# First image's group statistics formed and spread by TensorE instead of by way of DRAM

## The chip, the cores and the metric

The kernel runs on one core of a Trainium2 chip, as one launch. The metric is the device time of one execution in microseconds, as the median of several runs. All tensors are float32.

## The reference

Two layers of the same form act on four images of 32 x 32 positions with 768 channels. Each layer adds to its input the output of a multi-head self-attention (12 heads of 64) with relative position biases. The attention's input is normalized by groups of channels. Cut to what matters here:

```python
def _gn(v, G=32, eps=1e-5):
    g = v.reshape(B_, H_, W_, G, C_ // G)
    m = jnp.mean(g, axis=(1, 2, 4), keepdims=True)
    s = jnp.var(g, axis=(1, 2, 4), keepdims=True)
    return ((g - m) / jnp.sqrt(s + eps)).reshape(v.shape)

# attention of a layer, on the normalized input
qkv = x @ Wqkv                                # layer 1 also adds a bias
scores = scale * q @ k.T + bias               # bias[q, k] = rel_h + rel_w
out = softmax(scores) @ v
return out @ Wproj + bproj

x = x + _L0_conv_ref(_gn(x), ...)
x = x + _L1_conv_ref(_gn(x), ...)
```

A group is 24 neighbouring channels over all 1024 positions. Its variance is the mean of the 24 channels' variances plus the variance of their 24 means.

## The kernel before

An image is held with channels in the partitions: 768 channels are six blocks (`c`) of 128, and each block is two tiles of 512 positions (`h`). Layer and image together give eight images `im`, and each has six pairs of heads. A unit of the main loop is one pair and one block of 128 query positions (384 units). In a unit TensorE forms scores, VectorE adds the bias that GpSimd has written (L429), ScalarE takes the exponentials, VectorE transposes blocks of 32, two DMAs by way of DRAM complete the transposition, and TensorE weighs the values (`weigh`, L508). Beside this, TensorE projects queries, keys and values of the next pair (`products`, `project_values`, through `crossed`, L285) and the outputs. GpSimd forms combinations of weights (`combine`, L126) and of inputs (`sums`, L243), which the products use.

The order of the work is written out by hand under a manual schedule. What stands ahead of it, the loads and the tables of positions, is placed by the framework. The DMAs of weights and inputs are on SP's queue. Tiles come from rotating pools: `pt` and the PSUM pool `m` have two buffers each, `nrm` has two.

The work around the change is at the start, for image 0 alone. VectorE takes the statistics of each channel as the tiles land (`stats`, L188 and L191) and leaves mean and variance in `mv_of[0]`. Groups of 24 channels cross the partitions, and 128 is no multiple of 24, so the kernel sends the 768 x 2 numbers to DRAM (`gather`) and reads them back with a group in each of 32 partitions (`by_group`). VectorE and ScalarE form a factor and an offset for each group (`groups`, `inverses`). The two are copied 24 times, written to DRAM, and read back with a channel in each partition (`spread`). Then `apply` normalizes the twelve tiles in place, six on VectorE and six on ScalarE, and TensorE's first products begin:

```python
stages, apply = norm(0)
for n in sorted(stages):
    stages[n]()
for stage in range(2):
    combine(0, stage)
for h in range(2):
    for c in range(NC):
        apply(c, h, c % 2 == 1)
```

The four DMAs of image 0 are on ScalarE's queue. For images 1 to 7 the same stages run on SP's queue, spread over units of the pair before, and with other work beside them.

## Time and profile before

| | |
|---|---|
| median of 3 runs | 3404.13 us (3402.43 to 3408.83) |
| profiled execution | 3401.86 us, its span 3400.0 us |
| PE busy | 3324.9 us, 98% of the span |
| VectorE, ScalarE, GpSimd busy | 2347.4, 2090.8, 2332.3 us |
| chain that ended last | PE 81%, DMA 7%, DVE 4%, ACT 4% |
| last channel statistics end | 13.52 us |
| first normalization begins | 26.80 us |
| first matmul | 27.40 us |

The busy times are of the whole span; the last three rows are read from the chain of waits, with times from the span's start. The names PE, PEld, DVE, ACT, POOL and SP in the profile are TensorE's matmuls, its weight loads, VectorE, ScalarE, GpSimd and SyncE. L191 is line 191 of the kernel.

### The profile page before, as it was taken

The numbers are of one execution on the slowest core, as the hardware profiler recorded it, in microseconds if no ns is written. First come the engines' busy times: TensorE is split into PE (matmuls) and PEld (weight loads), VectorE is DVE, ScalarE is ACT, GpSimd is POOL, SyncE is SP. The second block draws the span as 40 slices with busy tenths as digits, with TensorE's granted clock in tenths as the row PEclk, the third lists the DMA queues.
The fourth block names the chain that finished last, engine by engine and source line by source line (L and its number), as shares of the span: only waits on it lengthen the run. The fifth ranks groups of instructions, "written<-read, shape, count | busy, mean of one in ns | idle before, by whom it ended". The sixth has DMA issues, their size and how long they took to land.

```text
span 3400.0 us, 58086 instructions
## 1 busy us (share of the span) xinstructions
PE 3324.9 (98%) x21600; PEld 1877.2 (55%) x21600; DVE 2347.4 (69%) x3826; ACT 2090.8 (61%) x3237; POOL 2332.3 (69%) x1184
## 2 busy tenths in 40 slices
PE   6999999999999999999999999999999999999998
PEld 3555555555555555555555555555555555555554
DVE  3776677766777666766767766666766676666675
ACT  2666756566566666566665666666666667665663
POOL 5776866668666686666866668666686667766662
PEclk9999999999999999999999999999999999999999
DMA  3898989999998998889888989989988999898887
GB/s 112 307 325 300 335 298 337 321 304 327 317 318 316 318 324 309 309 297 332 313 309 311 312 311 320 317 310 315 325 314 305 332 299 335 308 311 301 312 292 259
DMA packets 534777, 1046.97 MB, mean 308 GB/s; under 512 B 149728, under 2 KB 212704, under 8 KB 485344
## 3 DMA queue, kind: packets, MB, share of 16 engines
q1 hardware_dynamic: 479936, 1015.84, 85.3%
q10 hardware_dynamic: 54560, 27.43, 2.8%
q8 instruction: 171, 2.80, 0.3%
q14 instruction: 110, 0.90, 0.1%
HBM read 568.01 MB, written 475.10 MB: 307 GB/s over the span
## 4 chain that ended last, share of the span: by engine, by line
PE 81%; DMA 7%; DVE 4%; ACT 4%; issue 2%; POOL 1%; SPq 1%; ACTq 0%; DVEq 0%; POOLq 0%
PE pj L285 20%; PE s L443 16%; PE av L508 14%; PE pv L285 13%; PE oo L285 12%; DMA td<-tb 5%; PE pj L313 3%; PE tp L381 2%; DVE tb L479 2%; ACT sc L473 2%; POOL sc L429 1%; PE o L587 1%; ACT sc L459 1%; DMA xn<-in_x 1%; ACT xn L233 1%
## 5 line engine op out<-in xcount | busy, mean ns | idle before, releaser
L429 POOL TENSOR_TENSOR sc<-rel 128x1024 f32<-128x1024 f32 x768 | 1879.7, 2476 | 660.1 <-DVE tb L479 626.8
L455 DVE CUSTOM_DVE_ANT_0 sc<-s,sc 128x1024 f32<-128x1024 f32 x768 | 910.8, 1225 | 747.9 <-PE s L443 561.9
L459 ACT ACTIVATE sc<-sc,sm 128x1024 f32<-128x1024 f32 x768 | 878.7, 1146 | 472.0 <-DVE sm L455 471.0
L473 ACT ACTIVATE sc<-sc,sm 128x1024 f32<-128x1024 f32 x674 | 743.0, 1143 | 581.2 <-DVE sm L467 415.4
L479 DVE STREAM_TRANSPOSE tb<-sc 128x1024 f32<-128x1024 f32 x768 | 909.9, 1227 | 52.8 <-DMA td<-tb 44.7
L443 PE MATMUL s<-k,q 64*128 64x512 f32 x3072 | 738.3, 596 | 1.7 <-DVE sm L455 1.7
L508 PE MATMUL av<-pt,v 128*64 128x256 f32 x6144 | 685.5, 381 | 7.0 <-DMA pt<-td 6.0
L508 PEld LDWEIGHTS av<-pt,v 128*64 128x64 f32 x6144 | 434.8, 137 | 287.0 <-issue 45.0
L285 PE MATMUL pv<-wv,xn 64*128 64x256 f32 x4608 | 522.8, 376 | 1.0 <-DVE wv L274 1.0
L285 PEld LDWEIGHTS pv<-wv,xn 64*128 64x128 f32 x4608 | 447.3, 187 | 114.1 <-issue 56.9
L285 PE MATMUL oo<-attn,wo 64*128 64x512 f32 x2112 | 477.1, 591 | 0.0
L443 PEld LDWEIGHTS s<-k,q 64*128 64x128 f32 x3072 | 290.1, 187 | 313.7 <-issue 292.2
L285 PEld LDWEIGHTS oo<-attn,wo 64*128 64x128 f32 x2112 | 202.0, 188 | 228.7 <-issue 227.2
L471 POOL TENSOR_SCALAR sc<-sc,sm 128x1024 f32<-128x1024 f32 x94 | 105.1, 1118 | 311.8 <-DVE sm L467 310.8
L285 PE MATMUL pj<-xn,wa 64*128 64x512 f32 x1152 | 269.1, 598 | 33.2 <-DVE xn L235 27.4
L285 PE MATMUL pj<-xn,w 64*128 64x512 f32 x1152 | 263.4, 589 | 1.6 <-DVE w L274 1.6
L285 PE MATMUL pj<-s,w 64*128 64x512 f32 x576 | 262.7, 589 | 1.5 <-ACT attn L519 0.8
L285 PE MATMUL pj<-s,wc 64*128 64x512 f32 x576 | 262.8, 589 | 0.0
L285 PEld LDWEIGHTS pj<-xn,wa 64*128 64x128 f32 x1152 | 113.6, 189 | 168.9 <-issue 127.4
L285 PEld LDWEIGHTS pj<-xn,w 64*128 64x128 f32 x1152 | 112.4, 187 | 136.6 <-issue 134.1
L404 ACT COPY rel<-raw 32x256 f32<-32x256 f32 x384 | 155.1, 404 | 22.2 <-DMA part<-res 6.7
L285 PEld LDWEIGHTS pj<-s,wc 64*128 64x128 f32 x576 | 107.4, 187 | 67.0 <-issue 67.0
(68 smaller groups left out, 2111.4 us busy)
## 6 DMA issues: line engine op xcount, KB each, us to landing
td<-tb SPq DMA_DIRECT2D x384, 1024.0 KB, 6.5
pt<-td SPq DMA_DIRECT2D x382, 1024.0 KB, 8.9
tdr<-t ACTq DMA_DIRECT2D x96, 256.0 KB, 6.3
part<-res SPq DMA_DIRECT2D x84, 256.0 KB, 4.5
res<-part SPq DMA_DIRECT2D x84, 256.0 KB, 4.9
wa<-in_wqk SPq DMA_DIRECT2D x48, 384.0 KB, 3.2
wc<-in_wqk SPq DMA_DIRECT2D x48, 384.0 KB, 7.4
wv<-in_wv SPq DMA_DIRECT2D x24, 768.0 KB, 12.2
```

The lines of the kernel that those rows point to most:

```text
L285: nc.tensor.matmul(to, lhsT=w, rhs=x, start=(half, at) == (0, 0), stop=(half, at) == (1, n - 1))
L313: nc.tensor.matmul(t[:, h, :], lhsT=w[rows, c, :], rhs=x[c][rows, :], start=(c == 0), stop=(c == NB - 1),)
L381: nc.tensor.matmul(ps[:, h, j, :], lhsT=q[rows, at * P : (at + 1) * P], rhs=tabs[l][rows, :], start=True, stop=True,)
L404: nc.scalar.copy(rel[rows, :, 0, :, :], raw[rows, :, :, WIDE - 1 - HW - y : WIDE - 1 - y])
L429: nc.gpsimd.tensor_tensor(sc.rearrange("p (a k) (u l) -> p a (k u) l", a=4, l=8), rel[:, h, 0, m, :].unsqueeze(1).unsqueeze(3).to_broadcas ...
L443: nc.tensor.matmul(ps[h][:, cols], lhsT=q[rows, n * P : (n + 1) * P], rhs=k[rows, cols], start=True, stop=True,)
L455: nc.vector.tensor_tensor_reduce(out=sc, in0=ps[h], in1=sc, scale=-scale, scalar=BIG, op0=ALU.add, op1=ALU.min, accum_out=st[:, 0, h : h + 1],
L459: nc.scalar.activation(sc, sc, AF.Exp, bias=st[:, 0, h : h + 1], scale=-1.0, accum_out=st[:, 1, h : h + 1],)
L471: nc.gpsimd.tensor_scalar(sc, sc, st[:, 2, h : h + 1], 1.0, ALU.mult, ALU.mult)
L473: nc.scalar.mul(sc, sc, st[:, 2, h : h + 1])
L479: nc.vector.transpose(tb[:, :, h, :], sc_of[g, n, h])
L508: nc.tensor.matmul(av[rows, at * 2 * P : (at + 1) * 2 * P], lhsT=v_of[g][:, k, rows], rhs=pt_of[g, quarter].rearrange("p n r k h i -> p (n ...
```

## The change

Two masks of 0 and 1 are written by GpSimd at the very start, each 128 partitions x 6 x 128. The first, `of_group`, tells for each block of channels which group a channel is in (of 128 columns 32 stand for groups; the rest are empty). The second, `to_channel`, is its transpose by blocks. Each is a memset and two selects. They lie in a buffer of the pool `pt`.

For image 0 the stages by way of DRAM are replaced by four rounds of six matmuls. The first sums the channels' means by group. VectorE divides by 24, and the second round spreads the group's mean to its channels. VectorE forms each channel's variance plus the square of its distance from the group's mean. The third round sums these by group; VectorE and ScalarE form the factor and the offset; the fourth round spreads the two to the channels, and a copy puts them into `nrm`. For images 1 to 7 nothing changes but that SP's queue is now named directly. `apply` is moved into a function of its own.

```diff
+    masks = ptpool.tile([P, 2, 4, NT, 2, HW], FP, tag="pt", name="masks")
+    masks = masks.rearrange("p n r k h i -> p (n r k h i)")
+    of_group = masks[:, : NC * P].rearrange("p (c g) -> p c g", c=NC)
+    to_channel = masks[:, NC * P : 2 * NC * P].rearrange("p (c j) -> p c j", c=NC)
+    for mask, steps, per_row in ((of_group, (P, -GS), 1), (to_channel, (P, 1), -GS)):
+        nc.gpsimd.memset(mask, 1.0)
+        for sign, base in ((1, 0), (-1, GS - 1)):
+            nc.gpsimd.affine_select(
+                out=mask, in_=mask, pattern=[[sign * steps[0], NC], [sign * steps[1], P]],
+                compare_op=ALU.is_ge, fill=0.0, base=base, channel_multiplier=sign * per_row,
+            )
+
     for c in range(NC):
         for h in range(2):
             load_x(0, c, h)
...
+    def norm_first():
+
+        mv = mv_of[0]
+        w = small.tile([P, NC, 2], FP, tag="nrm", bufs=2, name="nrm_work")
+        nrm = small.tile([P, NC, 2], FP, tag="nrm", bufs=2, name="nrm_0")
+        ps = ps_m.tile([P, 2, HALF], FP, tag="m", name="groups_0")
+        total = [ps[:, 1, k : k + 1] for k in range(2)]
+
+        def by_group(to, x):
+            for c in range(NC):
+                nc.tensor.matmul(
+                    to, lhsT=of_group[:, c, :], rhs=x(c), start=(c == 0), stop=(c == NC - 1)
+                )
+
+        def by_channel(at, n, x):
+            for c in range(NC):
+                nc.tensor.matmul(
+                    ps[:, 0, at + n * c : at + n * (c + 1)], lhsT=to_channel[:, c, :], rhs=x,
+                    start=True, stop=True,
+                )
+
+        mean = small.tile([P, 2], FP, tag="gm", bufs=1, name="gm_0")
+        inv = small.tile([P, 2], FP, tag="gi", bufs=1, name="gi_0")
+        by_group(total[0], lambda c: mv[:, c, 0:1])
+        nc.vector.tensor_scalar(mean[:, 0:1], total[0], 1.0 / GS, None, ALU.mult)
+        by_channel(0, 1, mean[:, 0:1])
+        off, var = w[:, :, 0], w[:, :, 1]
+        nc.vector.tensor_tensor(off, ps[:, 0, :NC], mv[:, :, 0], ALU.subtract)
+        nc.vector.tensor_tensor(var, off, off, ALU.mult)
+        nc.vector.tensor_tensor(var, var, mv[:, :, 1], ALU.add)
+        by_group(total[1], lambda c: w[:, c, 1:2])
+        nc.vector.tensor_scalar(inv[:, 0:1], total[1], 1.0 / GS, EPS, ALU.mult, ALU.add)
+        nc.scalar.activation(inv[:, 1:2], inv[:, 0:1], AF.Sqrt)
+        nc.vector.reciprocal(inv[:, 0:1], inv[:, 1:2])
+        nc.vector.tensor_scalar(inv[:, 1:2], mean[:, 0:1], inv[:, 0:1], -1.0, ALU.mult, ALU.mult)
+        by_channel(NC, 2, inv)
+        nc.vector.tensor_copy(
+            nrm, ps[:, 0, NC : 3 * NC].rearrange("p (c k) -> p c k", c=NC)
+        )
+        return applied(0, nrm)
...
-        queue = nc.sync if im else nc.scalar
+        queue = nc.sync
...
-        stages, apply = norm(0)
-        for n in sorted(stages):
-            stages[n]()
+        apply = norm_first()
         for stage in range(2):
             combine(0, stage)
         for h in range(2):
```

More of the change, by code (lines that the diff above doesn't have):

```diff
@@ L191, in stats, with applied, apply @@
             nc.vector.bn_aggr(mv_of[im][:, c, :], st[:, c].rearrange("p i s -> p (i s)"))
+    def applied(im, nrm):
+        def apply(c, h, scalar=True):
+            x = xn_of[im][h][c]
+            if scalar:
+                nc.scalar.activation(x, x, AF.Identity, bias=nrm[:, c, 1:2], scale=nrm[:, c, 0:1])
+            else:
+                nc.vector.tensor_scalar(
+                    x, x, nrm[:, c, 0:1], nrm[:, c, 1:2], ALU.mult, ALU.add
+                )
+        return apply
+    def norm_first():
[32 more added lines that the diff above has]
+            nrm, ps[:, 0, NC : 3 * NC].rearrange("p (c k) -> p c k", c=NC)
+        )
+        return applied(0, nrm)
@@ L228, in spread @@
             queue.dma_start(out=nrm, in_=back.rearrange("(c p) s -> p c s", p=P))
-        def apply(c, h, scalar=True):
-            x = xn_of[im][h][c]
-            if scalar:
-                nc.scalar.activation(x, x, AF.Identity, bias=nrm[:, c, 1:2], scale=nrm[:, c, 0:1])
-            else:
-                nc.vector.tensor_scalar(
-                    x, x, nrm[:, c, 0:1], nrm[:, c, 1:2], ALU.mult, ALU.add
-                )
-        return {1: gather, 2: by_group, 4: groups, 5: inverses, 7: spread}, apply
+        return {1: gather, 2: by_group, 4: groups, 5: inverses, 7: spread}, applied(im, nrm)
     sum_tiles = {}
```

## The prediction

> **What bounds the kernel now.** I first read sections 1 and 4 of the page. TensorE is busy for 98% of the span, and the chain that ended last is 81% PE. So the kernel is bound by TensorE in its steady state, and a few small steps at the start can count only if they delay the first matmul: everything later is released by events, so a delay of the first matmul is carried to the end once, and no more than once. I therefore read the chain of waits in order of time over the first 100 us. The gap that the change addresses lies between these lines (start us, length us, what):

> ```profile
> 13.30 0.22 DVE mv L191
> ...
> 13.54 6.16 DMA per<-mv
> ...
> 19.78 1.81 DMA g<-per
> ...
> 22.54 0.21 ACT gmv L218
> ...
> 22.77 0.16 DVE gmv L221
> ...
> 23.39 1.34 DMA back<-g
> 24.73 0.02 issue
> 24.76 2.02 DMA nrm<-back
> 26.77 0.03 issue
> 26.80 0.56 DVE xn L235
> 27.36 0.04 issue
> 27.40 4.64 PE pj L285 x10
> ```

> From the end of the last channel statistics (13.52) to the first normalization (26.80) pass 13.28 us. Four DMAs take 6.16 + 1.81 + 1.34 + 2.02 = 11.33 us of it; small DVE and ACT instructions and the gaps take the other 1.95. Nothing else is on the chain there, and TensorE has not yet run.

> Then I asked the timelines of TensorE's weight loads and of GpSimd for the same stretch (start us, busy us, line, count, idle before):

> ```profile
> 29.27 0.45 PEld L285 LDWEIGHTS pj<-xn,wa 64*128 64x128 f32 x2 [0.40 <-issue]
> 30.12 0.45 PEld L285 LDWEIGHTS pj<-xn,wa 64*128 64x128 f32 x2 [0.40 <-issue]
> 30.96 0.25 PEld L285 LDWEIGHTS pj<-xn,wa 64*128 64x128 f32 x2 [0.39 <-issue]
> 31.39 0.19 PEld L285 LDWEIGHTS pv<-wv,xn 64*128 64x128 f32 x1 [0.18 <-issue]
> ```

> ```profile
> 0.72 0.35 POOL L156 MEMSET tab<- 128x128 f32 x2 [0.29 <-POOLq L882]
> 14.55 0.99 POOL L129 TENSOR_TENSOR w<-wc,wa 128x384 f32<-128x384 f32 x1 [13.49 <-DMA wc<-in_wqk]
> 19.96 0.53 POOL L166 TENSOR_SCALAR tab<-tab 128x128 f32<-128x128 f32 x1
> 28.80 4.13 POOL L257 TENSOR_TENSOR s<-xn,xn 128x512 f32<-128x512 f32 x3 [8.31 <-DVE xn L235]
> ```

> The loads show how fast TensorE is when it wakes: steps of 0.85 and 0.84 us until 30.96, then 0.43. For its first 3.5 us it runs at half speed. GpSimd is idle from about 1.1 to 14.5 us, and again from 20.5 to 28.8.

> [...] 27.40 to 30.96 at half speed. A second case bears on a chain with pauses: in the stretch from 70 to 80 us the mean granted clock is 0.66, after an idle 3.11 us at 70.0. [...]

> **The change, part by part.** Its own base is the profiled execution: 3401.86 us (span 3400.0 and 1.86 around it), which is 2.27 below the median of 3404.13. I work out a difference and apply it to the median.

> *Removed:* the 13.28 us above, with four ACT queue issues (0.40, 0.34, 0.31, 0.38 us), two of them followed by waits. ACT's table load (1.28 us at 20.16) stood behind them in ACT's queue; now ACT can do it in the first microseconds. It was hidden beside a DMA, and stays hidden.

> *Masks:* two memsets and four selects of 128x768 on GpSimd. A memset of 128 elements takes 0.20 and one of a single element 0.10, so 768 come to about 0.7 us. No select is in the trace. The cheapest near row is the GpSimd multiplication by a scalar (L471, 1118 ns for 1024), which gives 0.84 us for 768. [...] The first is needed at 13.5, the second at about 14.4. Their cover is GpSimd's idle time to 14.5; without it the group chain waits, and behind it the combinations of weights (4 x 0.99), the tables, and the sums.

> *TensorE's rounds:* the new chain has four: sum means by group, spread the mean, sum variances, spread the two factors. Each is six matmuls with 128x128 weights and one or two columns moving. The page counts two PE instructions for an fp32 matmul (pj from xn,wa: 1152 for 48 pairs of heads, so 24 where the code has 12), so a round is 12 loads and 12 tiny matmuls. What does one cost? The matmuls of tp (L381) are the nearest: weights of 128 columns too, 128 columns moving, 16 in 1.16 us on two row halves at once; (1.16 - 0.27) / 8 = 0.11 us a step. With one column moving the load must bind, and I keep 0.11 warm and 0.22 at half clock. Adding what the first load delays (0.14) and the last matmul's drain (0.20: a cold 1057 ns for 512 columns against a step of 853), a cold round takes 0.14 + 11 x 0.22 + 0.20 = 2.76 us, a warm one about 0.08 + 11 x 0.11 + 0.17 = 1.46. The first round is nearly off the path: five channel blocks are done before the last aggregate, so two loads and matmuls remain, 0.56 cold.

> *Small steps:* after round 1 one tensor_scalar (0.20, as L222); after round 2 three VectorE operations on 128x6 (0.20 each); after round 3 tensor_scalar 0.20, Sqrt 0.21, reciprocal 0.16, tensor_scalar 0.20; after round 4 a copy, 0.20. That is 1.77; ten handovers at 0.03 add 0.3.

> *Sum, cold:* 0.56 + 3 x 2.76 + 1.77 + 0.3 = 10.9 us against 13.28: a gain of **2.4 us**. If warm throughout: 0.4 + 3 x 1.46 + 2.1 = 6.9, a gain of 6.4. Is it cold? Busy rounds of 2.8 us alternate with pauses of 0.6 to 0.9, about 75 to 80% busy, mostly loads. After the stop at 70 us TensorE was still at half clock from 73.1 until about 78.6 (its 12 matmuls took 5.49 us against 2.7 warm), although it worked from 73.1 on. So I take cold, and keep the warm end for the range.

> *What is late next:* with normalization at 24.4 the first weights are there (issued at 7.3 to 9.1, 4.6 to 7.2 us to landing), and the combinations and tables end at 20.5 as before. The 12 sums keep their distance to the normalization; TensorE's queue holds them 3 us or more after they are ready (s2 ends at 40.3, its first matmul is at 43.66). Rotating one place in the pt, nrm and m buffers costs nothing: the masks, work tile and PSUM tile are read out before the next user comes; the last is released by the copy that itself precedes the normalization. No SP or POOL DMA moves, and per-image normalization of images 1 to 7 is unchanged on SP.

> **The rivals.** *TensorE wakes during the chain* (0.32): if the loads count as activity, rounds 3 and 4 run warm, the chain falls to about 8.3 (5.0 gained), and the first products, whose cold stretch to 30.96 then goes, come up to 0.9 us sooner by my count: the normalization still feeds them. With rounds warm from the start 7.3 in all, and 9 if the missing cold stretch at 72 us adds its 2.7. For it: the high duty. Against: the pauses. Time about 3397, 5 to 9 below before.

> *The masks are late* (0.19), the case on the other side. The second mask decides once it is ready later than 14.4 + 2.4 = 16.8 us: that is a select of over 3.6 us[...]. [...] For it: GpSimd takes 2.4 ns an element with two inputs, and no select is priced by a run. Against: 13 us of free time.

> *The gain is not passed on* (0.07): another start-up resource, such as GpSimd's sums or the DMA of rel, holds the first scores at 63.4. The chain has nothing but PE and its own followers up to there, so I doubt it; the time would be 3404, or a few microseconds more if half-clock loads cost 0.3 us a step (36 x 0.08 = 2.9 lost).

> **How the numbers follow.** The forecast (0.42) is 3404.13 - 2.4, rounded to 3401.7. A measurement of this kernel can tell about 0.2%, or 6.8 us, from no change; so the forecast is "same". Of the waking case I put 0.24 beyond that bound and 0.08 inside; of late masks 0.16 slower and 0.03 inside; of the third 0.05 inside and 0.02 slower. Faster 0.24, same 0.58, slower 0.18. The range goes from 3395.5 (waking, all of it) to 3407.5 (loads at 0.3 us a step, or masks a little late, with the 6 us between the shown runs in mind), and leaves out most of the late-mask case.

> **What would show it.** Right: no DMA between L191's last aggregate and the first normalization, that stretch 10 to 11.5 us long, weight-load steps of about 0.22 us in three rounds, masks done before 13.5, the first pj matmul near 25. Rounds of 1.5 us say that TensorE woke. A first spread matmul that waits for POOL says that the masks were late. The prediction is wrong if the stretch shrinks and the first scores (63.4) don't move with it, or if the time moves by more than the stretch does.

## The result, and the profile after

The changed kernel took 3394.36 us (median of 13 runs, 3386.99 to 3404.66), the kernel before 3403.6 (13 runs beside it, 3398.76 to 3409.07). The ratio is 0.9971, with a 95% interval of 0.9959 to 0.9982: faster by 0.3%, some 9 us where 2.4 were forecast, and below the forecast's range. With three more sets of runs of the same kernel (experiments; 73 runs in all, against 182 of the kernel before) it is 6.8 ± 1.4 us. Where a difference is given with ± here, it is that of the means of the runs, on one chip unless several sets are put together, with 1.96 standard errors. The changed kernel's profiled execution took 3389.95 us (span 3388.2).

The chain of waits after, at the place where the DMAs stood (start us, length us, what):

```profile
13.29 0.22 DVE mv L203
...
13.55 0.60 PE groups L228 x2
...
14.18 0.17 DVE gm L242
...
14.48 2.71 PE groups L234 x12
...
17.61 0.94 DVE nrm_work L247
...
18.59 2.73 PE groups L228 x12
...
22.25 2.73 PE groups L234 x12
...
25.01 0.18 DVE nrm L254
25.21 0.56 DVE xn L212
25.77 0.04 issue
25.82 5.61 PE pj L342 x10
```

No DMA is left between the last aggregate and the normalization. That stretch, 13.51 to 25.21, is 11.70 us long where it was 13.28: the normalization is 1.6 us sooner. Each full round lasts 2.7 us. In an experiment (`e12`) a round of twelve took 1.48 us at a granted clock of 1.00 and 2.73 at 0.50. By that comparison TensorE is at half clock here; this trace's own records of the clock begin only at 31.48 us.

The other microseconds are far from the edit. TensorE's timeline of the kernel before, behind the last scores (start us, busy us, engine, line, operation, count, and in brackets the idle time ahead and what ended it):

```profile
3341.84 2.27 PE L443 MATMUL s<-k,q 64*128 64x512 f32 x8
3345.11 3.67 PE L508 MATMUL av<-pt,v 128*64 128x256 f32 x32 [1.00 <-DVE sum L606]
3350.35 3.67 PE L508 MATMUL av<-pt,v 128*64 128x256 f32 x32 [1.57 <-DMA pt<-td]
3353.95 1.12 PE L587 MATMUL o<-attn,wa 128*128 128x512 f32 x2
```

and of the changed kernel:

```profile
3333.49 2.27 PE L500 MATMUL s<-k,q 64*128 64x512 f32 x8
3336.76 7.13 PE L565 MATMUL av<-pt,v 128*64 128x256 f32 x64 [1.00 <-DVE sum L663]
3343.82 1.13 PE L644 MATMUL o<-attn,wa 128*128 128x512 f32 x2
```

Before, the second half of these 64 matmuls waits 1.57 us for `pt`, the weights that come back from DRAM. After, it does not wait. From the last scores to the span's end are 53.28 us before and 49.80 after. Early on, the timeline before

```profile
67.83 2.16 PE L443 MATMUL s<-k,q 64*128 64x512 f32 x8
73.10 3.78 PE L285 MATMUL pj<-xn,wa 64*128 64x512 f32 x8 [3.11 <-DVE wa L274]
```

and after

```profile
67.30 2.16 PE L500 MATMUL s<-k,q 64*128 64x512 f32 x8
71.77 4.54 PE L342 MATMUL pj<-xn,wa 64*128 64x512 f32 x12 [2.31 <-DVE wa L331]
```

show a stop of 3.11 against 2.31 us. I therefore split each span at three points: the first scores (start of the first VectorE pass over them: 65.57 before, 65.04 after), from there to the ninth unit's scores (62.46 and 60.02), and behind the last scores (53.28 and 49.80). The two stretches differ by 2.4 and 3.5 us, the start by only 0.5. The middle, 3218.7 and 3213.3 us here, lies anywhere between 3210 and 3221 us in the twenty profiles of this case: it scatters by more than the whole gain. Nothing that the diff touches runs in these stretches, and on every engine the instructions follow in the same order there.

One thing does move. The page's list of DMA queues has this line, word for word the same in both kernels:

```profile
q8 instruction: 171, 2.80, 0.3%
```

These are 171 packets of 16 KB. By the queue's name I take them for reads of instructions, and call them reads. In the records they come, on average, at every 256th of TensorE's instructions (159 to 336 apart before, 170 to 361 after). The change puts 99 more TensorE instructions ahead of the first product (43,943 records in its two queues against 43,844; 96 of them are the four rounds), so every later read comes, on average, 99 instructions earlier in the work: the first three begin at 41.5, 64.5 and 88.4 us before, at 33.4, 50.1 and 81.6 after. This is what the experiments had to test.

### The profile page after: what moved, and what is told of

It is laid out like the page before. It is cut to its first block, busy times and chain, and to the rows that moved or that the text cites. A ratio compares the mean times of both kernels' runs of the same rounds, so it can differ in the third digit from the quotient of the medians.

```text
span 3388.2 us, 58184 instructions
## 1 busy us (share of the span) xinstructions
PE 3333.6 (98%) x21648; PEld 1894.1 (56%) x21648; DVE 2347.9 (69%) x3825; ACT 2090.1 (62%) x3237; POOL 2336.8 (69%) x1190
## 3 DMA queue, kind: packets, MB, share of 16 engines
q10 hardware_dynamic: 52896, 27.40, 2.7%
## 4 chain that ended last, share of the span: by engine, by line
PE 80%; DMA 9%; DVE 4%; ACT 3%; issue 2%; POOL 1%; SPq 1%; ACTq 0%; DVEq 0%; POOLq 0%
PE pj L342 19%; PE s L500 16%; PE av L565 14%; PE pv L342 13%; PE oo L342 12%; DMA td<-tb 6%; PE pj L370 3%; PE tp L438 2%; DVE tb L536 2%; ACT sc L530 2%; POOL sc L486 1%; PE o L644 1%; DMA xn<-mid 1%; DMA xn<-in_x 1%; ACT xn L210 1%
## 5 line engine op out<-in xcount | busy, mean ns | idle before, releaser
L536 DVE STREAM_TRANSPOSE tb<-sc 128x1024 f32<-128x1024 f32 x768 | 909.3, 1226 | 41.7 <-DMA td<-tb 33.4
L516 ACT ACTIVATION_READ_ACCUMULATOR sc<-sc,sm 128x1 f32 x768 | 144.4, 188 | 0.0
```

Of the source, the lines that this page charges most:

```text
L516: nc.scalar.activation(sc, sc, AF.Exp, bias=st[:, 0, h : h + 1], scale=-1.0, accum_out=st[:, 1, h : h + 1],)
L536: nc.vector.transpose(tb[:, :, h, :], sc_of[g, n, h])
```

## The experiments

**1. What counts: the scratch, the start, or something else?** `e1` is the changed kernel again. The first suspects were the DRAM addresses (the change removes two scratch tiles, so later scratch lies 16 KB lower) and the number of DMAs. `e2` restores both in the changed kernel, with nobody reading:

```diff
+        per = dram2.tile([C, 2], FP, tag="per", name="per_0")
+        back = dram2.tile([C, 2], FP, tag="back", name="back_0")
...
+        for to, x in unread:   # four, behind the normalization
+            nc.scalar.dma_start(out=to, in_=x)
```

`e3` delays the changed kernel's start by one more round, unread:

```diff
+        by_group(ps[:, 1, 2:3], lambda c: w[:, c, 1:2])
         by_group(total[1], lambda c: w[:, c, 1:2])
```

`e4` gives the kernel before the new addresses: for the first image `per` and `back` are parts of a tile that another user rotates through.

```diff
+            t_of[0] = dram2.tile([S, P], FP, tag="tdr", name="tdr_0")
+            per, back = t_of[0][:C, 0:2], t_of[0][:C, 2:4]
...
-        if i == 0:
+        if i == 0 and g:
```

> The changed kernel, unchanged, as a measure for the others of this call and for a second trace. All theories: 6 to 14 us below the kernel before, with the first scores about 0.5 us earlier. What it tells: which of the later steps of the difference (at 2053 and 3359 us in the first pair of traces) come back and which were chance.

> The changed kernel, and behind the normalization ScalarE's queue also writes four small unread DMAs into the two scratch tensors that the change had removed. Every later scratch tensor in DRAM then lies where it lay in the kernel before (16 KB higher than in the changed one), and the count of DMAs is the old one. Theory A, the gain comes from the start (an earlier first matmul, and what its new phase does to TensorE's clock later): still 9 us below the kernel before, within 3. Theory B, the gain comes from where the scratch lies in DRAM: at most 2 us below. Theory C, the new turn of the rotating PSUM, pt and statistics buffers: 9 us below, as A.

> The changed kernel with one more round of six matmuls ahead of the variances' round, its result unread. The normalization begins 2.7 us later, at about 27.9, and so 1.1 us later than in the kernel before. Theory A (the start): the gain is gone, 0 to 2 us above the kernel before. Theories B and C (scratch place, buffers): 2.7 us above the changed kernel, so 6 to 7 us below the kernel before.

> The kernel before, but the two small scratch tensors of image 0 lie inside the first 512 KB tensor of position products, which isn't written yet. All later scratch then lies in DRAM where it lies in the changed kernel, 16 KB lower; the way by DRAM and all rotating buffers stay. Theory B (scratch place): 7 to 9 us below the kernel before. Theories A and C: within 2 us of the kernel before.

Measured against the kernel before on this chip (mean 3402.4): `e1` −6.1 ± 2.4 us, `e2` −7.1 ± 2.2, `e3` −5.4 ± 2.6, `e4` +1.3 ± 3.5. The scratch's place is out, in both directions, and so is the count of DMAs. `e3` has its first scores 2.4 us later than the kernel before and is still 5.4 us faster: most of the gain is not the start.

**2. The place of the instruction reads.** `e5` adds 24 unread products (96 TensorE instructions) to the kernel before, while it waits for its statistics; `e7` and `e8` add 12 and 40 (48 and 160 instructions). `e6` adds 39 (156) to the changed kernel, which with its own 99 come to nearly 256, a full turn: the reads stand where they stood before.

```diff
+        d = [ps_m.tile([P, S], FP, tag="m", name=f"d{i}") for i in range(2)]
+        for i in range(24):   # e7: 12, e8: 40, e13: 64; e6 and e11: 39
+            x = xn_of[0][0][0]
+            nc.tensor.matmul(d[i % 2][:32, :1], lhsT=x[:, :32], rhs=x[:, :1], start=True, stop=True)
```

> The kernel before, with 24 tiny unread fp32 matmuls (96 TensorE instructions) ahead of its first product, done by about 12 us while TensorE is idle anyway; nothing else moves, and no address changes. The traces show 16 KB reads by the instruction queue at every 256th TensorE instruction; the change puts 99 TensorE instructions ahead of everything and so moves all of these reads against the data DMAs. Theory D, that shift is the larger part of the gain: 5 to 7 us below the kernel before, the first scores where they were. Theory C (the new turn of rotating buffers) and theory A (the start): within 2 us of the kernel before.

> The changed kernel, with 39 tiny unread matmuls (156 TensorE instructions) ahead of its first round, so that with the change's own 99 the shift comes to 255, next to a whole 256, and the instruction reads lie where they lay in the kernel before; the buffers' turn is that of the changed kernel. Theory D: 0 to 3 us below the kernel before. Theory C: 6 to 7 us below.

> The kernel before, with 12 tiny matmuls (48 instructions). Theory D: the time moves by some microseconds, up or down, and the last stall ahead of the last values (pt late by 1.6 to 2.5 us after the last scores, in the kernel before and in the one with new scratch) is gone or smaller, since no instruction read falls at 1.4 us after the last scores. Theories A and C: within 2 us of the kernel before, and the stall stays.

> The kernel before, with 40 tiny matmuls (160 instructions). Theory D: as for 48, the time moves by some microseconds in either direction; together with 0, 48 and 96 it shows how the time depends on the shift. Theories A and C: within 2 us of the kernel before.

Measured (mean before 3400.6): `e5` −2.1 ± 2.7, `e6` −2.5 ± 2.9, `e7` −0.4 ± 2.8, `e8` −0.2 ± 4.2. With the reads moved back, the changed kernel kept 2.5 of its 6.8 us. Moving them forward in the kernel before did not clearly shorten the time. The profiles say more, though each is of one execution, and those of `e5` and of its repeat `e10` below are the fastest of their 14 runs each. `e5` has the changed kernel's stretches (60.30 and 47.93 us) though it still goes by way of DRAM, and `e6` those of before (62.39 and 53.16). The waits of TensorE in `e6` (us, times, longest) have the old stop again

```profile
PE av L565 <- DMA pt<-td: 5.5, 5, 2.0
...
PE pj L342 <- DVE wa L331: 3.3, 1, 3.3
```

and in `e5` it is gone:

```profile
PE av L508 <- DMA pt<-td: 2.7, 3, 1.3
...
PE pj L285 <- DVE wa L274: 2.3, 1, 2.3
```

**3. Again, and TensorE awake.** Both shifts were run once more beside the changed kernel (`e9`). `e12` tests the forecast's rival: 64 unread products (64 columns moving) run ahead of the rounds in the changed kernel, so that TensorE is awake when they begin.

> The changed kernel again, on the chip of the next three, so that the parts can be set against each other there. Theory D: 5 to 8 us below the kernel before, its stretch behind the last scores 50 us long (53 to 54 in the kernel before).

> The kernel before with 96 TensorE instructions more ahead of its first product, as in e5, with the changed kernel beside it. Theory D: at least half of the changed kernel's gain (3 to 6 us below the kernel before), the rest being the earlier start. If the shift is not the cause: within 2 us of the kernel before while the changed kernel is 5 us or more below.

> The changed kernel with its instruction reads moved back, as in e6. Theory D: 3 to 6 us above the changed kernel, 1 to 3 below the kernel before, and again a stretch of 53 us behind the last scores. If the shift is not the cause: as the changed kernel.

> The changed kernel, with 64 unread matmuls (32 weight columns, 64 columns moving, 256 instructions, so a whole read's worth, and the reads lie as in the changed kernel) ahead of the first round, from about 4 to 13 us. They release TensorE's clock before the rounds begin. If the pauses of the chain are short enough to keep it released: rounds of 1.5 instead of 2.7 us, the normalization near 21.5 instead of 25.2, the first products at full speed, and the first scores 4 to 6 us earlier than in the changed kernel; the time 4 to 6 us below it. If small matmuls and weight loads don't count as activity: rounds of 2.7 us and no change.

Measured (mean before 3401.3): `e9` −7.1 ± 3.1, `e10` −1.3 ± 2.8, `e11` −2.5 ± 2.7, `e12` −6.2 ± 2.5. The answer is the same as in the first set: of some 7 us, reads moved back leave 2.5 (against `e9` on the same chip they cost 4.7 ± 3.6), and reads moved alone bring 1 to 2. `e12` has unread products too, but 256 instructions of them, a full turn, and keeps the gain: the products themselves are not what costs `e6` and `e11` theirs. In `e12` TensorE did not stay awake. The stretches of its profile (from:to us, length; busy us and counts of PE, PEld, DVE, ACT and POOL; then the granted clock, the DMA share and GB/s):

```profile
8.00:13.00 5.00, 5.00 (x86) 5.00 (x85) 4.20 (x10) 0.00 (x0) 0.00 (x0) 1.00 1.05 403
13.00:18.00 5.00, 4.02 (x30) 3.75 (x27) 1.85 (x6) 0.00 (x0) 2.76 (x3) 0.76 0.62 204
18.00:25.00 7.00, 5.44 (x24) 5.27 (x24) 1.04 (x6) 0.20 (x1) 1.93 (x4) 0.50 0.00 0
```

It was at full clock to 15.6 us, in the midst of the second round, and then at half clock through two rounds in which it was busy for 5.44 of 7 us. The first round took 1.48 us warm, the last two 2.73 as before.

**4. What else turns, and what the start is worth.** `e13` shifts the reads by 256 (64 products), a full turn. `e14` turns the rotating buffers (`pt`, `m`, `nrm` and the small tiles) by one place in the kernel before, as the change does, with one-column memsets. `e16` makes the rounds shorter, since a group of channels has only one of 32 rows (`inv`, and `mean` from its product with `to_channel` on, likewise on `:NG`):

```diff
-                    to, lhsT=of_group[:, c, :], rhs=x(c), start=(c == 0), stop=(c == NC - 1)
+                    to[:NG], lhsT=of_group[:, c, :NG], rhs=x(c), start=(c == 0), stop=(c == NC - 1)
...
-                    ps[:, 0, at + n * c : at + n * (c + 1)], lhsT=to_channel[:, c, :], rhs=x,
+                    ps[:, 0, at + n * c : at + n * (c + 1)], lhsT=to_channel[:NG, c, :], rhs=x,
```

`e17` is `e16` once more, and `e18` delays the changed kernel's chain on VectorE without touching TensorE's instructions:

```diff
+        for _ in range(48):
+            nc.vector.tensor_copy(mean[:, 1:2], mean[:, 0:1])
         nc.vector.reciprocal(inv[:, 0:1], inv[:, 1:2])
```

> The kernel before, with 64 tiny unread matmuls (256 TensorE instructions, exactly one read) ahead of its first product: a control for the cost of such matmuls, since all later instruction reads fall where they fell before. If they cost nothing: within 2 us of the kernel before. If they cost 2 to 3 us at the start, that is the part of the shift's gain which e5 and e10 did not show.

> The kernel before, with one dummy tile each in the pools of pt, PSUM m and nrm and two small ones, so that all rotating buffers stand as in the changed kernel; five one-column memsets on VectorE are all it adds. Theory C (the buffers' turn is worth what is missing): 2 to 4 us below the kernel before. Theory D without it: within 2 us.

> The changed kernel on the chip of these runs: 5 to 9 us below the kernel before, under every theory.

> The changed kernel, with 32 weight columns instead of 128 in the two rounds that sum by group, and 32 rows in the two that spread. The number of TensorE instructions is the same, so the reads stay. By the step seen in e5 (0.055 us for 32 columns at half clock, 0.22 for 128), the round of the variances takes 0.9 instead of 2.7 us, and the normalization begins at about 23.3 instead of 25.2. If a gain at the start is carried 1:1 to the end: 2 us below the changed kernel. [...]

> The shortened rounds of e16 again, on another chip. If the start is carried 1:1: 8 to 10 us below the kernel before (the changed kernel's 7 and 2 more). If e16's six runs were right: 12 to 15 us below.

> The changed kernel with 48 copies of one column on VectorE between the variances' round and the reciprocal, about 8 us on the chain. Carried 1:1: the first scores 8 us later than in the changed kernel and the time 8 us above it, so 0 to 2 us above the kernel before. If the start hardly matters, because something later waits anyway: still 4 to 7 us below the kernel before.

Measured (mean before 3401.7): `e13` −2.4 ± 3.7, `e14` −0.2 ± 2.8, `e15` (the changed kernel) −6.2 ± 2.3, `e16` −13.9 ± 4.2 from 6 runs; on the last chip (mean before 3402.9) `e17` −8.7 ± 2.9 and `e18` +2.2 ± 2.9. The turn of the buffers shows no gain. A full turn of the reads leaves the stretches as before (61.97 and 52.37). `e18` has its first scores 9.3 us behind the mean of the changed kernel's profiles (64.5) and lost 9.0 ± 3.2 (from −6.8 to +2.2): the start is carried to the end one to one. (`e3`, with its first scores 3.4 us behind that mean, lost only 1.4 ± 2.9, which the noise still allows.)

`e16` beats both kernels on its chip: 0.9957 (0.994 to 0.9974) of the kernel before, and 7.7 ± 4.3 us below the changed kernel. `e17`, at 0.9969 (0.9957 to 0.9982), beats the kernel before; its 8.7 ± 2.9 us are not clearly more than the changed kernel's 6.8 ± 1.4. The chain of waits of `e16` shows where it gains:

```profile
14.20 0.28 PE groups L228 x2
...
14.79 2.70 PE groups L234 x12
...
18.36 0.81 PE groups L228 x12
...
20.05 2.73 PE groups L234 x12
...
23.01 0.56 DVE xn L212
```

The rounds with 32 columns of weights fall to 0.28 and 0.81 us; those with 32 rows but 128 columns stay at 2.7. First scores come at 62.02 and 62.41, some 2.3 us before the changed kernel's. Carried one to one, that would give −6.8 − 2.3 = −9.1: `e17` fits, and `e16` is 4.8 us beyond it, a little more than its interval.

## Why the prediction was wrong

**What held.** The rounds: 2.71 to 2.73 us against 2.76 forecast, the short first one 0.60 against 0.56, and at half clock as chosen. The waking rival fell, and in `e12` dense work ahead of the rounds did not keep TensorE awake through them (granted clock 0.50 from 18 to 25 us). The masks were early: on GpSimd's timeline

```profile
0.79 1.41 POOL L147 MEMSET masks<- 128x768 f32 x2 [0.29 <-POOLq L937]
2.23 3.31 POOL L149 TENSOR_SCALAR_AFFINE_SELECT masks<-masks 128x768 f32<-128x768 f32 x4
5.49 0.34 POOL L168 MEMSET tab<- 128x128 f32 x2
14.43 0.99 POOL L129 TENSOR_TENSOR w<-wc,wa 128x384 f32<-128x384 f32 x1 [8.59 <-DMA wc<-in_wqk]
```

they end at 5.5 us, and after one more memset GpSimd stood idle for 8.6 us. A memset took 0.74 us (0.7 forecast), a select 0.86 (0.84 by the row of the multiplication by a scalar), and the selects begin as the memsets end. One of the tables of positions, forecast to end at 20.5, was formed only by 29.7, among the sums; nothing on the chain waited for it. "A delay of the first matmul is carried to the end once" held too (`e18`).

**One instruction was mis-sized.** The stretch of this profile is 11.70 us, not 10.9. VectorE's timeline has three operations of the same size in a row:

```profile
17.21 0.17 DVE L245 TENSOR_TENSOR nrm_work<-groups,mv 128x6 f32<-128x6 f32 x1 [2.88 <-PE groups L234]
17.41 0.17 DVE L246 TENSOR_TENSOR nrm_work<-nrm_work 128x6 f32<-128x6 f32 x1
17.61 0.93 DVE L247 TENSOR_TENSOR nrm_work<-nrm_work,mv 128x6 f32<-128x6 f32 x1
```

L247 was put at 0.20 and took 0.94. It ended at 18.54. GpSimd's last weight combination (L129, two inputs from SBUF) ran from 17.53 to 18.52. Both inputs of L247 lie in SBUF too, and it ended 0.02 us after the combination. In `e1`, `e3` and `e18` too the instruction of L247 began less than 0.1 us after that combination, took 0.95 to 0.99 us and ended 0.02 us after it. In `e2`, `e6`, `e9`, `e11` and `e15` it began up to 0.03 us before the combination and took 0.17. There the stretch is some 10.95 us, which is the forecast's 10.9, and `e9` and `e15` are the changed kernel itself. So the forecast of the stretch was right except for this one delay, which a few hundredths of a microsecond decide. The forecast priced the three instructions alike, at 0.20 each, without asking what GpSimd did beside them. What makes the one last until the other ends is not shown. In `e16`, whose chain runs a little later, it is L246 that takes 0.40.

**The start gave less than its stretch.** 1.6 us gained at the normalization were 0.5 at the first scores in the two profiles, since by the clock's records TensorE woke at 31.48 us after and at 30.94 before: it started its products sooner, but had 5.7 us of them at half clock instead of 3.5, so most of the gain went into slow products. In both traces the recorded changes of the clock lie 3.41 us or multiples of it apart, but not at the same times from the span's start: the next are to half, from 71.90 to 78.73 before and from 72.44 to 75.85 after. Over the four profiles of the changed kernel (65.04, 64.66, 64.13 and 64.18, mean 64.5) the start gains 1.1 us on the 65.57 before (65.11 and 65.87 in `e4` and `e14`, whose start is that of the kernel before).

**The step that failed** is the sentence that only a delay of the first matmul can count "and no more than once", with every other edit costed at nothing. The prediction named its own refutation: the time moves by more than the stretch does, 6.8 us against 1.6. It left out that 99 instructions more on TensorE's queue shift its instruction reads against the data transfers. With the reads back in their old place and all else of the change kept, 2.5 ± 2.0 us of the gain remain (`e6` and `e11` together), about what was forecast; 4.3 ± 2.4 are gone.

How a read costs is clearest at the stop of TensorE after the first scores. A DMA of 256 KB takes `t` to DRAM there; in the chain of waits before

```profile
64.14 3.10 DMA tdr<-t
```

and after

```profile
63.61 2.30 DMA tdr<-t
```

In the kernel before, a read begins at 64.47, inside this transfer. In all five profiles with a read 0.3 to 0.9 us behind the issue of this DMA, 2.8 to 3.3 us pass from it to the issue of the DMA that reads the result back, and TensorE's stop grows with it; in the fifteen others it is 2.3 us:

| reads | kernels | TensorE's stop, us | first scores to ninth unit's, us | behind the last scores, us |
|---|---|---|---|---|
| as before, one in the transfer | before, `e6`, `e11`, `e13`, `e14` | 2.78 to 3.31 | 61.97 to 63.16 | 50.06 to 53.28 |
| as before, that one 0.9 us ahead of the issue | `e4` | 2.31 | 60.63 | 54.27 |
| as after | after, `e1`, `e2`, `e5`, `e9`, `e10`, `e12`, `e15` to `e18` | 2.31 to 2.33 | 59.84 to 60.85 | 47.94 to 52.81 |
| in other places | `e3`, `e7`, `e8` | 2.32 | 59.75 to 59.95 | 49.44 to 52.85 |

Kernels with the DMA chain and kernels with TensorE's rounds stand on both sides, so it is not the edit itself. The first stretch parts cleanly, by some 2 us, and follows the stop. The last stretch does not part: with the reads as after it is 47.94 to 50.43 us in eight profiles, but 51.56 to 52.81 in `e12`, `e16` and `e17`.

For the last stretch, single packets show what a read may do. In the kernel before a read came 1.4 us after the last scores began, in the midst of the transfer that ends the wait of 1.57 us. Thirteen of that transfer's 16 parts landed at 0.2 to 1.0 us, the last three at 1.9, 3.1 and 3.5. In the changed kernel no read is near (23 us before, 15.6 after) and all 16 are there by 1.3. TensorE's next load of weights from this transfer came at 3.6, 0.1 us behind the last part: three late parts held it up. But it is not shown that the read made them late: `e13` has a read at 1.3 us and all 16 parts by 1.0, and `e16` has no read near and four parts at 2.35 to 3.26.

**What stays open.** The size in the time, first. The place of the reads is worth 4.3 ± 2.4 us in the changed kernel and 1.7 ± 1.9 in the kernel before (`e5` and `e10` together; `e7` gains 0.4 ± 2.8 and `e8` 0.2 ± 4.2, though the first stretch of all four is short). The two differ by 2.6 ± 3.1 us, so the runs do not tell whether the reads are worth the same in both kernels or help only beside the rounds. The first scores of `e5`, `e7`, `e8` and `e10` come 0.3 to 1.9 us later than before, which takes a part of their gain. Then the middle: most of the 171 reads fall there, and what they do is hidden in its scatter. And the late parts at the end: `e8`, `e12`, `e16` and `e17` have a stall of 0.7 to 1.3 us there with no read beside it, and `e11`, `e13` and `e14` have reads within 1.4 us and no stall. Shown, then, is that the place of one read, with no more than unread products added, lengthens one transfer, TensorE's stop behind it and the first stretch, and that moving the reads back costs the changed kernel 4.3 ± 2.4 of its 6.8 us. That the reads are the whole of the unforeseen gain is not shown.

A caution on size: 6.8 us is 0.2% of this kernel, and the first comparison happened to show more than the later three (7.1, 6.2 and 6.1 us). A gain of 6.8 us on the 3404.13 that the forecast starts from would have given 3397.3, inside its range, but by luck: that part of the range was meant for a TensorE that wakes, and it did not wake.

## What to carry to other kernels

When a short edit adds or removes TensorE instructions in a kernel like this, the reads, here one at every 256th on average, move against the data transfers everywhere behind; leave a few microseconds for it in the range (4.3 ± 2.4 here), and test it with unread instructions that make up the full turn. For small operations on VectorE with two SBUF inputs, ask what GpSimd reads at that moment (L247 took 0.94 us instead of 0.17). Before believing a small gain, split the span at fixed points of the work and see whether the gain lies where the edit is. For sums over groups by TensorE, cut the columns of the weights to what is needed: the loads, and not the columns moving, made up the round (2.73 us with 128 columns of weights and 0.81 with 32, but 2.71 and 2.73 with one and two columns moving).
